# A cheaper elu on ScalarE, the transposes' copies moved ahead, a third tile for v and earlier weight loads in a two-layer kernel

## The chip, the cores and the metric

The kernel runs on one core of a Trainium2 chip. A core has five engines with a queue of instructions each: TensorE (PE; its weight loads are shown apart as PEld), VectorE (DVE), ScalarE (ACT), GpSimd (POOL) and SyncE (SP), which here only issues transfers. DMA engines move the data between HBM and the core's memory SBUF; TensorE writes to a second memory, PSUM. The metric is the time of one execution in microseconds (us), as the median of several runs.

## The reference

The input x has 4 batches of 512 tokens with 128 numbers each. Two layers follow, each of the form `x = x + attention(norm(x)) * silu(experts(norm(x)))`. The change lies in the first layer. Its attention has 16 heads and goes over each batch in 8 segments of 64 tokens with a memory M and a normalizer Z carried from segment to segment:

```
scores = where(mask, -inf, q @ k.T * scale)
att_dot = softmax(scores) @ v
sq = elu(q) + 1;  sk = elu(k) + 1
att_mem = (sq @ M) / (sq @ Z.T)
M, Z = M + sk.T @ v, Z + sk.sum(rows)
out = (gate * att_mem + (1 - gate) * att_dot) @ Wo
```

`elu(x) + 1` is `exp(x)` for x below zero and `x + 1` above. The first layer's second half is a mixture of 8 experts, two of which each token uses, beside a shared one. The second layer has an attention over 16 phases and another mixture of 8 experts.

## The kernel before

All work is written out in Python for one core, and every engine carries it out in the written order: the helpers `act1`, `vec1`, `mm1` and `pool1` put an instruction at the place in its engine's queue where the program calls them. So an instruction that waits holds up everything behind it on its engine.

`load_first` (L119 to L166) issues the first loads. The 16 tiles of x go out first, four on ScalarE's queue and twelve on SP's; the experts' weights wg, wu and wd and then the attention's weights follow on SP's. `norm_ffn0` (from L386) makes the norms and runs the first layer's experts; it lasts until about 78 us.

`attn0` (from L579) is the first attention. It runs over 32 segments, 8 for each of the 4 batches. q and k are produced by `project` for four segments at a time, in chunks: a chunk is 16 matmuls into one PSUM bank (`pp`), copied out by ScalarE (`pj`); v takes four chunks (`pv`), copied to a tile `vt` (by VectorE for the first two groups, by ScalarE later), sent to DRAM as `vd` and read back in another layout as `vone`. The tiles `vt` come from a pool with two buffers, so the third copy waits until the first transfer has landed.

In iteration n of the main loop (the two lists below are the order on the engines):

- TensorE: `sc` (scores of segment n+1), `mm` (memory of n), `tn` (transposes: the attention of n-2 and elu(k) of n+1), `mu` (memory's update of n), `dot` (weights of n times v), then up to four chunks of `pp` or `pv`, or, in each fourth segment, the output projection `po`.
- DVE: `E` (scores capped, L666), `rm` and `t` (memory divided, L723 and L724), `elu` of q(n+1) (L689), `mz` (memory's update, L758), `rd` twice, `t` (attention divided) and `sums` (L777, L723, L724, L780), `elu` of k(n+2) (L689).
- ScalarE: exp and Relu of q(n+1) (`elu_exp`), four copies `attT` and one `sk` out of `tn`, exp and Relu of k(n+2), the copy of the first chunk, the exponential of `E`, the copies of the other chunks.
- POOL: `t` times the gate (L743), `t` times the other gate (L781), the sum of both (L782); after each output projection, the addition to x (L809).

PSUM holds four double banks that `sc`, `mm`, `tn`, `mu`, `dot` and the chunks take in turn. So each of them waits until what stood in its bank four places earlier has been copied out.

elu is made of three instructions: ScalarE makes exp(x) and max(x, 0), and DVE adds min(exp(x), 1) and max(x, 0) in one. In the last segment of a batch (n = 7, 15, 23, 31) the memory isn't updated, so that k has no elu there and there is no `mu` and no `mz`.

From segment 18 on, the loop also carries steps of the second layer's experts for the first two batches (`between`): norm sums in 18 and 19, a square root on ScalarE in 20 with a table load on either side of it, the scaled tiles `xn` in 20 and 21, routing in 23 to 25. Chunks end with segment 25; segments 26 to 31 have none.

Of the kernel before, what the change touches and what calls it, by code (L numbers as in the profile page):

```python
# [12 lines left out]
F32 = mybir.dt.float32  # L13
# [3 lines left out]
AF = mybir.ActivationFunctionType  # L17
ALU = mybir.AluOpType
# [3 lines left out]
P = 128  # L22
B, S, D = 4, 512, 128
# [3 lines left out]
NT = 16  # L27
# [81 lines left out]
class Kernel:  # L109
# [8 lines left out]

    def load_first(self, pool, pool_attn, crossed=False):  # L119
        nc, i = self.nc, self.i  # L120
        for n in range(NT):
            eng = nc.scalar if n in (1, 3, 5, 7) else nc.sync
            eng.dma_start(out=self.x[:, n, :], in_=self.tiles_of(i["L0_attn_x"], n))

        self.wr = pool.tile([P, NE], F32, name="wr")
        nc.gpsimd.dma_start(out=self.wr, in_=i["L0_ffn_Wr"])
        self.ebias = pool.tile([P, NE], F32, name="ebias")
        nc.gpsimd.dma_start(out=self.ebias, in_=i["L0_ffn_expert_bias"].partition_broadcast(P))
        self.sg = pool.tile([P, 128], F32, name="sg")
        nc.gpsimd.dma_start(out=self.sg, in_=i["L0_ffn_Sg"])  # L130
        self.su = pool.tile([P, 128], F32, name="su")
        nc.gpsimd.dma_start(out=self.su, in_=i["L0_ffn_Su"])
        self.sd = pool.tile([P, D], F32, name="sd")
        nc.gpsimd.dma_start(out=self.sd, in_=i["L0_ffn_Sd"])
        self.wg = pool.tile([P, NE, F0], F32, name="wg")
        nc.sync.dma_start(out=self.wg, in_=i["L0_ffn_Wg"].rearrange("e d f -> d e f"))
        self.wu = pool.tile([P, NE, F0], F32, name="wu")
        nc.sync.dma_start(out=self.wu, in_=i["L0_ffn_Wu"].rearrange("e d f -> d e f"))
        self.wd = pool.tile([P, NE // 2, D], F32, name="wd")
        nc.sync.dma_start(  # L140
            out=self.wd, in_=i["L0_ffn_Wd"].rearrange("(j e) f d -> (e f) j d", e=2)
        )

        self.wqkv = []
        for w in ("Wq", "Wk", "Wv"):
            t = pool_attn.tile([P, H0 * DK], F32, name=f"l0{w}")
            nc.sync.dma_start(out=t, in_=i[f"L0_attn_{w}"])
            self.wqkv.append(t)
        self.wo = pool_attn.tile([P, H0, D], F32, name="l0wo")
        for p in range(2):  # L150
            nc.sync.dma_start(
                out=self.wo[p * 64 : p * 64 + 64],
                in_=i["L0_attn_Wo"].rearrange("(c v) d -> v c d", v=DK),
            )
        be = i["L0_attn_betas"][0, :, 0].rearrange("(hp a p) v -> a p hp v", a=2, p=2)
        self.gate = pool_attn.tile([P, 4, 2, DK], F32, name="gate")
        for p in range(2):
            for a in range(2):


                for x in range(2):
                    rows, cols = (a, slice(x, 4, 2))
                    if crossed:
                        rows, cols = (a + x) % 2, slice(2 * a, 2 * a + 2)
                    nc.sync.dma_start(
                        out=self.gate[rows * 64 : rows * 64 + 64, cols, p, :],  # L166
                        in_=be[a, p, x:4:2].partition_broadcast(64),
                    )
# [410 lines left out]
    def attn0(self, xnT, g0, stack, between):  # L579
# [4 lines left out]
        nc, tc = self.nc, self.tc  # L584
# [4 lines left out]
        pool = stack.enter_context(tc.tile_pool(name="a0", bufs=2))  # L589
# [9 lines left out]
        for k in range(4):  # L599
            t = pool.tile([P, 4, 2, DK + 1], F32, name=f"vone{k}", bufs=1)  # L600
            nc.gpsimd.memset(t[:, :, :, DK : DK + 1], 1.0)
            vone.append(t)
        qkv, vd, attT, seg = {}, {}, {}, {}
        wide = self.wide

        def project(h):


            if h >= 2 * B:
                return []  # L610
            qkv[h] = dst = [
                pool.tile([P, 32, 64], F32, name=f"pj{h}_{wi}", tag=f"pj{wi}")
                for wi in range(2)
            ]
            vd[h] = drams.tile([2, P * 16, DK], F32, name=f"vd{h}", tag="vd")
            def chunk_v(p, k):
                ps = self.narrow(f"pv{h}_{p}_{k}")
                self.mm1(
                    ps, lhsT=xnT[h // 2][:, h % 2 * 2 + p, :],
                    rhs=self.wqkv[2][:, k * S : (k + 1) * S], start=True, stop=True,  # L620
                )
                t = pool.tile([P, S], F32, name=f"vt{h}_{p}_{k}", tag="vt")
                if h > 1:
                    self.act1(t, ps, AF.Copy)
                else:
                    self.vec1(nc.vector.tensor_copy(t, ps))
                nc.sync.dma_start(
                    out=vd[h][p].rearrange("(q k c) d -> k q (c d)", k=2, c=8)[k], in_=t
                )

            def chunk(wi, cq):
                ps = self.narrow(f"pp{h}_{wi}_{cq}").rearrange("p (c k) -> p c k", c=4)
                for c4 in range(4):
                    c = cq * 4 + c4
                    for p in range(2):
                        self.mm1(
                            ps[halves[p], c4, :],
                            lhsT=self.wqkv[wi][:, c * 64 : c * 64 + 64],
                            rhs=xnT[h // 2][:, h % 2 * 2 + p, :], start=True, stop=True,
                        )  # L640
                view = dst[wi].rearrange("d k (t c) -> d (k t) c", c=16)
                self.act1(
                    view[:, :, cq * 4 : cq * 4 + 4], ps.rearrange("d c k -> d k c"), AF.Copy
                )
            qk = [(lambda wi=wi, cq=cq: chunk(wi, cq)) for wi in (1, 0) for cq in range(4)]
            v = [(lambda p=p, k=k: chunk_v(p, k)) for p in range(2) for k in range(2)]
            return v + qk if h else qk[:4] + v + qk[4:]

        def blocks(n, w):
            s = n % 4  # L650
            return qkv[n // 4][w][:, s * 8 : s * 8 + 8, :]
# [24 lines left out]
        def last(n):  # L676
            return n % 8 == 7

        def elu_exp(n, w):
            t = pool.tile([P, 8, 64], F32, name=f"elu{w}{n}", tag=f"elu{w}")  # L680
            up = pool.tile([P, 8, 64], F32, name=f"up{w}{n}", tag="up")
            self.act1(t, blocks(n, w), AF.Exp)
            self.act1(up, blocks(n, w), AF.Relu)
            seg[n][w] = t, up

        def elu(n, w):

            t, up = seg[n][w]
            self.vec1(nc.vector.scalar_tensor_tensor(t, t, 1.0, up, ALU.min, ALU.add))  # L689
            seg[n][w] = t  # L690
# [18 lines left out]
        def values(n):  # L709

            for p in range(2):
                src = vd[n // 4][p].rearrange("(s hp r) d -> s r hp d", s=4, hp=4)
                nc.sync.dma_start(out=vone[n % 4][:, :, p, 0:DK], in_=src[n % 4])
# [120 lines left out]
        for n in range(nseg):  # L834
            if n % 4 == 3:
                todo = project((n + 1) // 4 + 1)
            elif n == 0:
                todo = ahead
            each = 2 if n == 0 else 4 if n < 3 or n % 4 != 2 else 0
            nxt = n + 1 < nseg  # L840
            more = nxt and not last(n + 1)
            if n + 2 < nseg:
                values(n + 2)
            if nxt:
                elu_exp(n + 1, 0)
                scores(n + 1)
            memory(n)
            if nxt:
                elu(n + 1, 0)
            if n > 1 or more:  # L850
                turned(n - 2 if n > 1 else None, n + 1 if more else None)
            if not last(n):
                update(n)
            for f, *args in between.get(n - 0.5, []):
                f(*args)
            attend(n)
            ahead = n + 2 < nseg and not last(n + 2)
            if ahead:
                elu_exp(n + 2, 1)
            chunks, todo = todo[:each], todo[each:]  # L860
            for chunk in chunks[:1]:
                chunk()
            if nxt:
                scores_exp(n + 1)
            if ahead:
                elu(n + 2, 1)
            for chunk in chunks[1:]:
                chunk()
            for f, *args in between.get(n - 0.25, []):
                f(*args)  # L870
            if n % 4 == 2 and n > 4:
                output(n // 4 - 1)
            if not nxt:
                turned(n - 1)
            for f, *args in between.get(n, []):
                f(*args)
# [1611 lines left out]
```

## Time and profile before

| | us |
|---|---|
| median of 3 runs | 711.25 (709.93 to 712.07) |
| profiled execution | 715.14 |
| its span in the profile | 713.4 |
| TensorE busy | 667.3 |
| VectorE busy | 498.2 |
| ScalarE busy | 488.8 |
| GpSimd busy | 342.5 |

The span is divided, roughly, into the first layer's experts (to 78 us), the first attention (78 to 318), the second layer's experts (318 to 425) and its attention (425 to 713). A line of the profile names the engine, the line of the kernel and the tiles (`out<-in`), with busy time and mean duration in ns. Where the helpers record an operation, the line is that of the helper (L336 for all matmuls, L339 for all of ScalarE's activations), so these are told apart by their tiles. A releaser (`<-`) is what ended an idle time. Instructions of one engine overlap a little: a VectorE instruction shown with 0.69 us lets the next begin after about 0.61.

### The profile page before, as it was taken

What the parts mean: (1) busy time and instruction counts of PE and PEld (TensorE: products, weight loads), DVE (VectorE), ACT (ScalarE), POOL (GpSimd) and SP (SyncE); (2) the same over time, 40 slices, a digit from 0 to 9 for tenths busy, and PEclk for the clock granted to TensorE, in tenths of its full rate; (3) what the DMA queues carried; (4) which work ended last, traced back from release to release, by engine and by line L of the source; (5) the groups of instructions that cost most, each with busy time, mean ns of one, the idle gap of its engine ahead of it and who ended that gap; (6) DMA issues with size and microseconds to landing.
All of it is one profiled execution on the core that took longest, in us unless ns stands there. A gap on an engine that the chain in (4) does not pass through costs nothing.

```text
span 713.4 us, 23787 instructions
## 1 busy us (share of the span) xinstructions
PE 667.3 (94%) x10128; PEld 414.4 (58%) x10131; DVE 498.2 (70%) x1078; ACT 488.8 (69%) x809; POOL 342.5 (48%) x381
## 2 busy tenths in 40 slices
PE   7999899999999799789999999999999999999994
PEld 3666667977977668667777774332335243422433
DVE  5876475675677658864379125889897999588854
ACT  3423477786886977643453369989977999899830
POOL 7670046667667475783653243312482753312240
PEclk9999999999999998999999999999999999999998
DMA  7740152232232121100034159877949484965200
GB/s 159 162 137 0 49 161 83 58 107 77 62 103 78 51 81 43 33 3 1 1 120 155 52 170 259 206 186 168 238 144 217 125 233 143 216 149 125 60 17 19
DMA packets 84849, 79.46 MB, mean 111 GB/s; under 512 B 42512, under 2 KB 73520, under 8 KB 81664
## 3 DMA queue, kind: packets, MB, share of 16 engines
q1 hardware_dynamic: 81904, 75.12, 40.1%
q0 software_dynamic: 2256, 2.47, 1.8%
q8 instruction: 82, 1.34, 0.8%
q10 hardware_dynamic: 576, 0.26, 0.2%
q14 instruction: 31, 0.25, 0.1%
HBM read 51.62 MB, written 26.21 MB: 109 GB/s over the span
## 4 chain that ended last, share of the span: by engine, by line
PE 67%; ACT 14%; DVE 12%; DMA 3%; issue 2%; SPq 1%; ACTq 0%; DVEq 0%
PE acc L336 10%; ACT e L339 8%; PE eo L336 7%; PE pp L336 6%; PE po L336 6%; PE ph L336 4%; PE b L336 4%; PE s L336 3%; PE pl L336 3%; PE pg L336 2%; PE pu L336 2%; PE den L336 2%; PE pv L336 2%; DMA vd<-vt 2%; PE sc L336 2%
## 5 line engine op out<-in xcount | busy, mean ns | idle before, releaser
L339 ACT ACTIVATE e<-s 128x1024 f32<-128x1024 f32 x124 | 121.9, 1055 | 13.6 <-PE s L336 12.4
L336 PE MATMUL acc<-e,strip 128*32 128x512 f32 x1000 | 124.0, 598 | 0.9 <-DVE e L1885 0.9
L339 ACT ACTIVATE e<-e 128x1024 f32<-128x1024 f32 x104 | 107.3, 1094 | 0.0
L743 POOL TENSOR_TENSOR t<-t,gate 128x512 f32<-128x512 f32 x32 | 50.2, 1568 | 54.7 <-DVE t L724 54.7
L336 PEld LDWEIGHTS acc<-e,strip 128*32 128x32 f32 x1000 | 28.5, 109 | 69.9 <-issue 58.7
L781 POOL TENSOR_TENSOR t<-t,gate 128x512 f32<-128x512 f32 x32 | 49.6, 1551 | 33.9 <-DVE sums L780 27.1
L689 DVE SCALAR_TENSOR_TENSOR elu<-elu,up 128x512 f32<-128x512 f32 x60 | 46.2, 770 | 11.0 <-ACT up L339 10.8
L339 ACT ACTIVATE pj<-pp 128x512 f32<-128x512 f32 x64 | 37.8, 610 | 14.6 <-PE pp L336 13.5
L339 ACT ACTIVATE h<-ph 128x1024 f32<-128x1024 f32 x20 | 20.5, 1024 | 39.7 <-PE ph L336 32.3
L336 PE MATMUL s<-q,k 64*128 64x512 bf16 x256 | 40.9, 382 | 3.5 <-ACT e L339 3.3
L782 POOL TENSOR_TENSOR t<-t,t 128x512 f32<-128x512 f32 x32 | 42.6, 1332 | 2.5
L336 PEld LDWEIGHTS <-k 64*128 64x128 bf16 x256 | 8.8, 94 | 59.6 <-issue 57.7
L666 DVE TENSOR_TENSOR E<-sc,cap 128x512 f32<-128x512 f32 x32 | 22.0, 688 | 28.7 <-PE sc L336 28.7
L336 PE MATMUL eo<-w_out,h 128*128 128x128 f32 x320 | 39.7, 278 | 0.0
L336 PEld LDWEIGHTS eo<-w_out,h 128*128 128x128 f32 x320 | 37.6, 192 | 3.4 <-issue 2.2
L339 ACT ACTIVATE elu<-pj 128x512 f32<-128x512 f32 x60 | 38.6, 643 | 0.1
L1725 POOL TENSOR_TENSOR pr<-pr,pr 128x512 f32<-128x512 f32 x14 | 22.6, 1631 | 33.0 <-DVE pr L1720 32.9
L339 ACT ACTIVATE up<-pj 128x512 f32<-128x512 f32 x60 | 38.4, 640 | 0.0
L336 PE MATMUL pp<-xnT,l0Wk 128*64 128x128 f32 x512 | 32.2, 282 | 2.8 <-ACT sk L339 2.0
L339 ACT ACTIVATE attT<-tn 128x128 f32<-128x128 f32 x100 | 19.5, 283 | 21.6 <-PE tn L702 20.8
L1168 POOL TENSOR_SCALAR th<-th 128x512 f32<-128x512 f32 x4 | 3.4, 840 | 63.9 <-ACT th L339 63.9
L1634 DVE TENSOR_TENSOR second<-second,first 128x1024 f32<-128x1024 f32 x16 | 27.0, 1694 | 9.3 <-DMA second<-qf 9.3
(337 smaller groups left out, 1625.8 us busy)
## 6 DMA issues: line engine op xcount, KB each, us to landing
vd<-vt SPq DMA_DIRECT2D x32, 256.0 KB
vone<-vd SPq DMA_DIRECT2D x64, 128.0 KB
first<-qe SPq DMA_DIRECT2D x8, 1024.0 KB
second<-qf SPq DMA_DIRECT2D x16, 512.0 KB
third<-qf SPq DMA_DIRECT2D x32, 256.0 KB
qf<-qT SPq DMA_DIRECT2D x64, 64.0 KB
k<-kd SPq DMA_DIRECT2D x16, 256.0 KB
q<-qd SPq DMA_DIRECT2D x16, 256.0 KB
```

What stands on the lines that cost most here:

```text
L336: return self.pin(self.nc.tensor.matmul(*args, **kw))
L339: return self.pin(self.nc.scalar.activation(*args, **kw))
L666: self.vec1(nc.vector.tensor_tensor(e, ps[:, :, 0:256].rearrange("p x (hp c) -> p x hp c", hp=4), bc(bc(self.cap, 1, 4), 1, 2), ALU.min,))
L689: self.vec1(nc.vector.scalar_tensor_tensor(t, t, 1.0, up, ALU.min, ALU.add))
L743: nc.gpsimd.tensor_mul(t, t, self.gate)
L781: nc.gpsimd.tensor_mul(t, t, gate2)
L782: nc.gpsimd.tensor_add(t, t, seg[n]["t1"])
L1168: self.pool1(self.nc.gpsimd.tensor_scalar(t, t, 0.5, 0.5, ALU.mult, ALU.add))
L1634: self.vec1(self.nc.vector.tensor_mul(t, t, self.first1[mm][:, two]))
L1725: self.nc.gpsimd.tensor_add(self.prod1[b, m], self.prod1[b, m], t)
```

## The change

Five things are changed:

- In `load_first`, the tiles 8 to 15 of x are issued behind wg and wu.
- `vt` has three buffers.
- For segments 2 to 26 (`short`), elu is made differently: DVE takes min(x, 0) into the tile (`elu_low`), ScalarE makes its exponential in place, and DVE adds max(x, 0) in one instruction. Relu on ScalarE falls away, and one instruction on DVE is added.
- The order changes. On DVE the minimum of q(n+1) stands ahead of `E`, that of k(n+2) behind the first `t`; the closing elu of q(n+1) moves from behind the first `t` to behind `sums`, right ahead of the elu of k(n+2). On ScalarE `attT` and `sk` come first, then the exponential of q(n+1); the exponential of k(n+2) comes behind that of `E`.
- For the other segments (0, 1 and 27 to 31) elu is made as before, but the exp and Relu of q(n+1) also come behind `attT` and `sk`, and those of k(n+2) behind the exponential of `E`.

TensorE's and POOL's instructions and their order stay as they are.

```diff
@@ load_first
-        for n in range(NT):
-            eng = nc.scalar if n in (1, 3, 5, 7) else nc.sync
-            eng.dma_start(out=self.x[:, n, :], in_=self.tiles_of(i["L0_attn_x"], n))
+        def tokens(first, end):
+            for n in range(first, end):
+                eng = nc.scalar if n in (1, 3, 5, 7) else nc.sync
+                eng.dma_start(out=self.x[:, n, :], in_=self.tiles_of(i["L0_attn_x"], n))
+        tokens(0, 8)
...
         self.wu = pool.tile([P, NE, F0], F32, name="wu")
         nc.sync.dma_start(out=self.wu, in_=i["L0_ffn_Wu"].rearrange("e d f -> d e f"))
+        tokens(8, NT)
         self.wd = pool.tile([P, NE // 2, D], F32, name="wd")
@@ chunk_v
-                t = pool.tile([P, S], F32, name=f"vt{h}_{p}_{k}", tag="vt")
+                t = pool.tile([P, S], F32, name=f"vt{h}_{p}_{k}", tag="vt", bufs=3)
@@ attn0
+        def short(n):
+            return 1 < n < 27
+
+        def elu_low(n, w):
+            if short(n):
+                seg[n][w] = pool.tile([P, 8, 64], F32, name=f"elu{w}{n}", tag=f"elu{w}")
+                self.vec1(nc.vector.tensor_scalar_min(seg[n][w], blocks(n, w), 0.0))
+
         def elu_exp(n, w):
+            if short(n):
+                self.act1(seg[n][w], seg[n][w], AF.Exp)
+                return
             t = pool.tile([P, 8, 64], F32, name=f"elu{w}{n}", tag=f"elu{w}")
...
         def elu(n, w):
 
+            if short(n):
+                t = seg[n][w]
+                self.vec1(nc.vector.scalar_tensor_tensor(t, blocks(n, w), 0.0, t, ALU.max, ALU.add))
+                return
             t, up = seg[n][w]
             self.vec1(nc.vector.scalar_tensor_tensor(t, t, 1.0, up, ALU.min, ALU.add))
...
@@ the loop
+            ahead = n + 2 < nseg and not last(n + 2)
+            if nxt:
+                elu_low(n + 1, 0)
+                scores(n + 1)
+            memory(n)
+            if ahead:
+                elu_low(n + 2, 1)
+            if n > 1 or more:
+                turned(n - 2 if n > 1 else None, n + 1 if more else None)
             if nxt:
                 elu_exp(n + 1, 0)
-                scores(n + 1)
-            memory(n)
-            if nxt:
-                elu(n + 1, 0)
-            if n > 1 or more:
-                turned(n - 2 if n > 1 else None, n + 1 if more else None)
+                if not short(n + 1):
+                    elu(n + 1, 0)
             if not last(n):
                 update(n)
...
             attend(n)
-            ahead = n + 2 < nseg and not last(n + 2)
-            if ahead:
-                elu_exp(n + 2, 1)
+            if nxt and short(n + 1):
+                elu(n + 1, 0)
...
             if nxt:
                 scores_exp(n + 1)
             if ahead:
+                elu_exp(n + 2, 1)
                 elu(n + 2, 1)
```

## The prediction

> **What bounds the kernel now.** I read the page's busy shares first, then the stages, then the chain that ended last, and then the instructions in order of time in the stages that the change touches.
>
> The page's first part: TensorE is busy 94% of the span, so work taken from ScalarE pays only where TensorE waits for it.
>
> ```profile
> PE 667.3 (94%) x10128; PEld 414.4 (58%) x10131; DVE 498.2 (70%) x1078; ACT 488.8 (69%) x809; POOL 342.5 (48%) x381
> ```
>
> The busy time by stage (columns: length, then PE, PEld, DVE, ACT, POOL). The first row is four segments of the first attention: TensorE idles 0.6 us, DVE has 7.6 us free, POOL 7.5. In the second, where the next layer's norms join in, TensorE idles 5.7; in the third, the last segments, 4.9.
>
> ```profile
> 138.00:165.00 27.00, 26.42 (x754) 22.66 (x756) 19.36 (x42) 21.67 (x53) 19.46 (x14) 1.00 0.30 82
> ...
> 219.00:254.00 35.00, 29.32 (x776) 23.17 (x772) 25.86 (x71) 26.01 (x58) 19.37 (x16) 1.00 0.25 66
> ...
> 288.00:318.00 30.00, 25.11 (x777) 21.66 (x774) 23.25 (x51) 16.03 (x44) 24.49 (x18) 0.94 0.09 21
> ```
>
> Waits from 103 to 291 us (total, times, longest): TensorE waits for ScalarE 8.2 us in all, half of it for the copy of sk. That is what the relief of ScalarE can bring at most.
>
> ```profile
> PE pp L336 <- ACT sk L339: 4.1, 6, 2.1
> PE dot L336 <- ACT vt L339: 2.7, 3, 1.4
> ```
>
> One plain segment on DVE and on POOL. Start to start gives what each costs in a row: E 0.61, rm 0.30, t 0.61, elu 0.60, mz 0.60, rd 0.19 and 0.24, t 0.61, sums 0.08, elu 0.60. POOL's products show 1.66 us where they begin under an elu, against 1.29 elsewhere: after the elu has ended they need 1.13.
>
> ```profile
> 155.82 0.69 DVE L666 TENSOR_TENSOR E<-sc,cap 128x512 f32<-128x512 f32 x1 [1.61 <-PE sc L336]
> ...
> 158.97 0.69 DVE L724 TENSOR_TENSOR t<-dot,rd 128x512 f32<-128x512 f32 x1
> 159.58 0.17 DVE L780 TENSOR_TENSOR sums<-rd,sums 128x16 f32<-128x16 f32 x1
> 159.66 0.68 DVE L689 SCALAR_TENSOR_TENSOR elu<-elu,up 128x512 f32<-128x512 f32 x1
> 162.29 0.69 DVE L666 TENSOR_TENSOR E<-sc,cap 128x512 f32<-128x512 f32 x1 [1.95 <-PE sc L336]
> ```
>
> ```profile
> 157.50 1.66 POOL L743 TENSOR_TENSOR t<-t,gate 128x512 f32<-128x512 f32 x1 [0.76 <-DVE t L724]
> 159.81 1.67 POOL L781 TENSOR_TENSOR t<-t,gate 128x512 f32<-128x512 f32 x1 [0.65 <-DVE sums L780]
> 161.55 1.29 POOL L782 TENSOR_TENSOR t<-t,t 128x512 f32<-128x512 f32 x1
> ```
>
> What decides this forecast: DVE instructions with tensors in SBUF alone, back to back, while POOL has products to do. A tensor_scalar of 0.34 us takes 1.46 behind the product at 248.34, and the elu at 298.03 takes 1.61 behind that at 297.82. POOL gets in between two such DVE instructions.
>
> ```profile
> 246.79 0.34 DVE L945 TENSOR_SCALAR xn<-x,mv,rstd 128x128 f32<-128x128 f32 x1
> 246.93 1.33 POOL L781 TENSOR_TENSOR t<-t,gate 128x512 f32<-128x512 f32 x1 [4.84 <-DVE t L724]
> 248.26 1.46 DVE L945 TENSOR_SCALAR xn<-x,mv,rstd 128x128 f32<-128x128 f32 x1
> 248.34 1.29 POOL L782 TENSOR_TENSOR t<-t,t 128x512 f32<-128x512 f32 x1
> ...
> 297.82 1.27 POOL L782 TENSOR_TENSOR t<-t,t 128x512 f32<-128x512 f32 x1
> 298.03 1.61 DVE L689 SCALAR_TENSOR_TENSOR elu<-elu,up 128x512 f32<-128x512 f32 x1
> ```
>
> At the start, TensorE waits 2.12 us for wg, which is issued at 8.94 behind twelve tiles of x; the chain holds this transfer for 4.98 us.
>
> ```profile
> 13.96 2.03 PE L336 MATMUL pg<-xnT,wg 128*128 128x512 f32 x2 [2.12 <-DMA wg<-in_L_ffn_Wg_dram]
> ...
> 14.00:17.50 3.50, 3.50 (x5) 1.27 (x6) 1.79 (x6) 0.64 (x2) 1.46 (x3) 0.51 1.11 243
> ```
>
> **The change, part by part.** The profiled execution took 715.14 us (span 713.4), 3.9 above the median of 711.25; the sum is made on the profile and carried over as a difference.
>
> *Weights sooner: -2.8.* Eight issues of 0.65 us leave SP's queue ahead of wg, which is then issued at 3.75 instead of 8.94 and, at the 4.98 us it took, lands at about 8.7; wu 0.6 later. TensorE needs wg at 11.83, so its wait goes. Late next is DVE: parts until 14.17, hs until 14.77, the four xn until 15.79. Then the transposes (0.6) and pg for the second pair begin near 16.5 instead of 19.30. The eight tiles of x moved behind wg and wu go out from 5.0 to 10.2, and their first reader, at 19.67, comes to 17: covered by some 4 us. wd keeps its place as the fifteenth issue, at 10.2; its reader at 20.6 comes to 18. POOL's and ScalarE's queues keep their order. From 19 to 78 us the chain is TensorE without a gap, so the gain stays. Bounds: 2.1 (the wait alone) and 3.7 (all up to 17.64 but 1.9 of work); I take what DVE leaves. The granted clock of 0.51 from 14.0 to 17.5 follows a gap of only 2.12 us, so the half-rate stretch should go as well. The Trainium skill (TensorE: Matmul & The Clock Gate, What's actually happening) has the clock halve after an idle window of about 3.4 us; by that this gap would not have halved it, and the gain would be the wait alone, 2.1.
>
> *Elu by a minimum, in a plain segment.* For 25 q and 22 k (segments 2 to 26, k not in the last of a sequence) a Relu leaves ScalarE: 47 x 0.64 us, off the path except in the waits above. DVE gets 47 minima. The nearest row is the tensor_scalar at L595, 128x512 in SBUF: 0.43 us alone, some 0.35 in a row; behind a POOL product it waits up to 1.13 more. The elu of q now stands behind t, next to the elu of k and the next segment's minimum: three instructions in SBUF in a row, while POOL has its product and sum of the same segment waiting. As at 246.79, POOL gets in after the first and after the second: elu q 0.60, product 1.13, elu k 0.60, sum 1.13, minimum 0.35, and only then E. The minimum of k, right behind t, goes ahead of POOL at 0.35. Per segment: 0.61+0.30+0.61+0.35+0.60+0.19+0.24+0.61+0.08+0.60+1.13+0.60+1.13+0.35 = 7.40 us. TensorE needs about 6.5 (four groups of pp 3.64, sc 0.62, mm 0.47, tn 0.64, mu 0.63, dot 0.47). So DVE becomes the bound. Without k (segments 5, 13) it is 5.3 and I take 5.5; without mz (7, 15) 6.8. The ends for the two waits are 0 and 2.26; I take the upper one, since the xn row has the same pattern.
>
> The Trainium skill (SBUF — State Buffer, Who interferes with whom) says that whoever issues first holds the port pair for the whole instruction. Read as DVE's queue going first, a segment would cost 5.14 and TensorE stay the bound; the xn row shows POOL taking its turn.
>
> *Sum by segments.* Segment 0: q of segment 1 keeps exp and Relu but now behind the copy of sk, +0.35; the first minima and a sum ahead of E(2) bring it to +1.25. Segment 1: 7.4 against 6.06, +1.3. Segments 2 to 17, from E at 107.41 to 216.34: 12x7.40 + 2x6.80 + 2x5.5 = 113.4 against 108.9, +4.5; the third tile of v and the copies first are in this, their waits being covered now by DVE. Segment 18 (norm sums, in POOL's shadow): +0.4. Segments 19 to 26 (to 292.07) had ScalarE and DVE in turn on the chain: +1.7 in 19 and +1.1 in 25, where two or three minima and a wait of 1.13 come on top of a full DVE; -1.4, -1.7 and -0.5 in 20, 21 and 22 to 24, where the wait for v (1.4 at TensorE) and the copy of sk behind the table loads (2.06) go: -0.8.
>
> *Segments 27 to 31: +3.7.* Here q keeps exp and Relu, but they now stand behind attT (0.65 in a row) and sk (0.49): ready 2.35 us after tn, at 295.47 instead of the elu at 293.59. Behind that elu queue mz, rd, t, the elu of k, and tn of the next segment. E(29) comes 1.9 later, E(30) 2.9 (the late elu now meets POOL's product), E(31) 4.0; the last po 3.7.
>
> Sum: -2.8 +1.25 +1.3 +4.5 +0.4 -0.8 +3.7 = +7.55 on the profile, 722.7; carried to the median 711.25 + 7.55 = 718.8.
>
> **The rivals.** *POOL's turns cost nothing (faster).* Were the two waits 0, TensorE would stay the bound: -2.8 weights, -8.2 waits for ScalarE, +0.6 at the start, +2.0 minima on the full DVE in 19 to 26, +2.5 tail: -5.9, 705.4. For it: POOL is busy 72% in a plain segment and could have finished. Against: xn. It decides if the two waits together stay under 1.3 us per segment (6.5 less 5.14).
> *Gains and costs meet (same).* Were the two waits 0.83 us each, the products being under way already, a plain segment would take 6.8; twelve of them at 0.6 less give 711.6. For it: ScalarE may have exp of k late, so that the elu of k meets POOL's product halfway. Against: the sum then waits behind that elu in full, ahead of the minimum.
> *The clock (slower still).* DVE-bound, TensorE idles near 0.9 us per segment. If that lets the clock drop as at 14.0, each 3.4 us at half costs up to 1.7; four of them make 725.5. Against: gaps of 0.7 at 114 and 178 did not; from 266 to 273 it stood at 0.54.
> *The weights do nothing.* Were wg late for other reasons, 2.8 more on any case.
>
> **How the numbers follow.** Forecast 0.52 (714 to 723 by itself), faster rival 0.27, same 0.07, clock 0.14. Slower by over 0.3% (2.1 us, about what a measurement of this kernel tells from none) is 0.52 + 0.14. The range reaches from 705, the faster rival, to 726.
>
> **What would show it.** Right: E to E near 7.4 us in plain segments, elu of k and the minimum of q with means far above 0.68 and 0.43, DVE on the chain from 100 to 290; E(29) to E(31) 5.5 to 6.5 apart; pg at 11.9 without a wait. Wrong: po still every 26.5 us with minima at 0.43 on the mean.

## The result and the profile after

The changed kernel takes 721.53 us (718.53 to 721.84, 4 runs) against 710.59 (709.89 to 712.07, 4 runs) for the kernel before: a ratio of 1.0133, 95% interval 1.0109 to 1.0157. It is slower by some 10.9 us in the median (9.5 by the ratio); the forecast was 718.8 with a range from 705 to 726. The profiled execution took 721.83 us, with a span of 720.1.

Busy time in the same four plain segments' stage as before, then in the last segments (columns: length, PE, PEld, DVE, ACT, POOL, granted clock, DMA share, GB/s):

```profile
138.00:165.00 27.00, 25.45 (x714) 21.28 (x714) 25.79 (x46) 16.62 (x43) 18.88 (x13) 1.00 0.30 81
...
300.00:330.00 30.00, 23.08 (x652) 20.06 (x650) 19.84 (x43) 15.68 (x41) 17.99 (x15) 0.77 0.05 12
```

The window is the same, but the changed kernel gets less done in it (714 matmuls for 754). ScalarE has 5 us less to do there, DVE went from 19.4 of 27 us to 25.8, and TensorE lost a microsecond. The page's chain, by engine, says the same of the whole span: DVE held 12% of it before.

```profile
PE 58%; DVE 25%; ACT 14%; issue 2%; DMA 1%; DVEq 0%; SPq 0%; ACTq 0%
```

The page's groups of the closing elu and of the minimum (busy us, mean ns of one) show that the DVE time is mostly not work. Alone they take 0.68 and 0.42 us.

```profile
L704 DVE SCALAR_TENSOR_TENSOR elu<-pj,elu 128x512 f32<-128x512 f32 x47 | 48.9, 1054 | 7.2 <-ACT elu L342 7.2
L688 DVE TENSOR_SCALAR elu<-pj 128x512 f32<-128x512 f32 x47 | 36.9, 784 | 0.5 <-ACT pj L342 0.5
```

One plain segment on DVE in order of time (start, duration), and then on POOL:

```profile
156.86 0.68 DVE L669 TENSOR_TENSOR E<-sc,cap 128x512 f32<-128x512 f32 x1
...
158.36 0.42 DVE L688 TENSOR_SCALAR elu<-pj 128x512 f32<-128x512 f32 x1
...
160.34 0.17 DVE L798 TENSOR_TENSOR sums<-rd,sums 128x16 f32<-128x16 f32 x1
160.43 0.68 DVE L704 SCALAR_TENSOR_TENSOR elu<-pj,elu 128x512 f32<-128x512 f32 x1
161.39 1.40 DVE L704 SCALAR_TENSOR_TENSOR elu<-pj,elu 128x512 f32<-128x512 f32 x1 [0.28 <-ACT elu L342]
162.71 1.51 DVE L688 TENSOR_SCALAR elu<-pj 128x512 f32<-128x512 f32 x1
164.15 0.68 DVE L669 TENSOR_TENSOR E<-sc,cap 128x512 f32<-128x512 f32 x1
```

```profile
160.57 1.67 POOL L799 TENSOR_TENSOR t<-t,gate 128x512 f32<-128x512 f32 x1 [0.65 <-PE pp L339]
162.32 1.62 POOL L800 TENSOR_TENSOR t<-t,t 128x512 f32<-128x512 f32 x1
```

DVE and POOL take turns: elu of q, POOL's product, elu of k, POOL's sum, the minimum, and only then E. The product ends at 162.24 and elu of k at 162.79; the sum ends at 163.94 and the minimum at 164.22. E to E is 7.29 us here. The step at the start came too; pg begins without a wait, and the second pair 3.2 us earlier than before:

```profile
11.28 1.02 PE L339 MATMUL pg<-xnT,wg 128*128 128x512 f32 x2
...
16.09 1.02 PE L339 MATMUL pg<-xnT,wg 128*128 128x512 f32 x2
```

### The profile page after: what moved, and what is told of

The parts are those of the page before. It is cut to its first block, busy times and chain, and to the rows that moved or that the text cites. A ratio compares the mean times of both kernels' runs of the same rounds, so it can differ in the third digit from the quotient of the medians.

```text
span 720.1 us, 23825 instructions
## 1 busy us (share of the span) xinstructions
PE 669.9 (93%) x10128; PEld 418.6 (58%) x10131; DVE 546.7 (76%) x1125; ACT 466.1 (65%) x762; POOL 345.8 (48%) x381
## 4 chain that ended last, share of the span: by engine, by line
PE 58%; DVE 25%; ACT 14%; issue 2%; DMA 1%; DVEq 0%; SPq 0%; ACTq 0%
PE acc L339 10%; ACT e L342 8%; PE eo L339 7%; DVE elu L704 4%; PE po L339 4%; PE pp L339 4%; PE ph L339 4%; DVE elu L688 4%; DVE t L742 3%; PE s L339 3%; PE b L339 3%; PE pl L339 3%; DVE E L669 2%; PE pg L339 2%; PE den L339 2%
## 5 line engine op out<-in xcount | busy, mean ns | idle before, releaser
L761 POOL TENSOR_TENSOR t<-t,gate 128x512 f32<-128x512 f32 x32 | 43.7, 1367 | 73.4 <-DVE t L742 73.4
L799 POOL TENSOR_TENSOR t<-t,gate 128x512 f32<-128x512 f32 x32 | 51.2, 1601 | 29.0 <-DVE sums L798 20.7
L704 DVE SCALAR_TENSOR_TENSOR elu<-pj,elu 128x512 f32<-128x512 f32 x47 | 48.9, 1054 | 7.2 <-ACT elu L342 7.2
L800 POOL TENSOR_TENSOR t<-t,t 128x512 f32<-128x512 f32 x32 | 48.1, 1505 | 2.5
L1748 POOL TENSOR_TENSOR pr<-pr,pr 128x512 f32<-128x512 f32 x14 | 22.6, 1635 | 32.0 <-DVE pr L1743 32.0
L688 DVE TENSOR_SCALAR elu<-pj 128x512 f32<-128x512 f32 x47 | 36.9, 784 | 0.5 <-ACT pj L342 0.5
L339 PEld LDWEIGHTS po<-l0wo,attT 64*128 64x128 f32 x512 | 31.6, 200 | 3.6 <-issue 2.4
L339 PE MATMUL po<-l0wo,attT 64*128 64x128 f32 x512 | 33.0, 287 | 0.6 <-DVE t L742 0.6
L339 PE MATMUL dot<-vone,E 64*64 64x65 f32 x1024 | 24.1, 237 | 9.9 <-DVE E L669 7.4
```

The costliest lines, as they stand in the source:

```text
L339: return self.pin(self.nc.tensor.matmul(*args, **kw))
L688: self.vec1(nc.vector.tensor_scalar_min(seg[n][w], blocks(n, w), 0.0))
L704: self.vec1(nc.vector.scalar_tensor_tensor(t, blocks(n, w), 0.0, t, ALU.max, ALU.add))
L761: nc.gpsimd.tensor_mul(t, t, self.gate)
L799: nc.gpsimd.tensor_mul(t, t, gate2)
L800: nc.gpsimd.tensor_add(t, t, seg[n]["t1"])
```

## The experiments

The theory of the prediction: in a plain segment DVE is the bound, because POOL's product and its sum get in between DVE instructions that stand in a row and have their tensors in SBUF. The rivals: the minima cost by their work alone; ScalarE's new order makes the exponentials late. Beside these stands the question what each of the other parts is worth. All ratios are to the kernel before on the same chip; the kernel before took 708.4 to 712.8 us on the chips used, so times of different runs are best compared by their ratios. "A plain segment" is the usual distance from one E to the next where k has an elu, and E(2) to E(18) are sixteen segments: 108.5 us in the profile before, 113.8 in the changed kernel.

**POOL's product and sum left out of the changed kernel.** The gate on the second part and the memory part are then missing.

```
-            nc.gpsimd.tensor_mul(t, t, gate2)
-            nc.gpsimd.tensor_add(t, t, seg[n]["t1"])
```

> The changed kernel with POOL's second product and its sum left out of every segment of the first attention, so that the attended values lack the gate on the second part and the whole memory part. DVE and ScalarE keep all their work and their order. Theory (DVE is held by POOL's turns between elu of q, elu of k and the minimum): elu of k and the minimum go back to 0.6 to 0.7 and 0.35 to 0.45 us, plain segments to TensorE's 6.5 us instead of 7.28, and the total falls by 12 x 0.78 in segments 2 to 17 and 2 to 4 in 19 to 31, some 11 to 13 us: 709. Rival (the 47 minima as work, or the later exponential, hold the segment): plain segments stay at 7.0 or above and the total above 717.

Measured: 703.90 us (699.37 to 708.24, 8 runs), ratio 0.9904 (0.9873 to 0.9934). DVE has all its 47 minima and ScalarE its new order. The groups of DVE from 80 to 340 us:

```profile
L704 DVE SCALAR_TENSOR_TENSOR elu<-pj,elu 128x512 f32<-128x512 f32 x47 | 32.2, 695 | 11.5 <-ACT elu L342 11.4
L688 DVE TENSOR_SCALAR elu<-pj 128x512 f32<-128x512 f32 x47 | 19.6, 418 | 0.9 <-ACT pj L342 0.9
```

The means fell from 1054 and 784 to 695 and 418 ns. Most plain segments take 6.4 to 6.5 us, E(2) to E(18) 106.6. So POOL's two instructions are what DVE was held by. Against the changed kernel's ratio of 1.0133 this is 2.3%, some 16 us, more than the 11 to 13 expected: E(18) to E(27), where 2 to 4 had been allowed for all that follows, fell by 7.4 us.

**The exponential of k back in its place.**

```
+            if ahead:
+                elu_exp(n + 2, 1)
             if nxt and short(n + 1):
                 elu(n + 1, 0)
...
             if ahead:
-                elu_exp(n + 2, 1)
                 elu(n + 2, 1)
```

> The changed kernel with the exponential of k put back to its place of before, ahead of the chunk of the projection and of the scores' exponential on ScalarE. Rival (the elu of k is late because its exponential is late: 0.28 us of its 1.40 show that wait): plain segments fall from 7.28 by 0.3 to 0.6, the total by 5 to 9 us. Theory (POOL's turn behind elu of q ends after the exponential anyhow): plain segments 7.2 to 7.35, total within 2 us of 721.5.

Measured: 721.87 us (717.20 to 724.94, 4 runs), ratio 1.0131 (1.0086 to 1.0175), plain segments 7.27 to 7.29, but for one of 8.08. The wait of 0.28 us that the trace puts down to the exponential lies inside POOL's turn and is worth nothing. For the exponential of k this rival is out; the rest of ScalarE's order is tried by itself further down.

**The minimum of q behind E.**

```
             if nxt:
-                elu_low(n + 1, 0)
                 scores(n + 1)
+                elu_low(n + 1, 0)
```

> The changed kernel with one edit: the minimum of q goes from ahead of E to just behind E, both neighbours then reading PSUM; elu of q and elu of k stay next to each other. Theory: of the two turns of 1.13 us the second is no longer in a chain of SBUF-only instructions, E begins behind elu of k: 5.14 + 1.13 = 6.27, again TensorE's 6.47; E(2) to E(18) 104 to 107, total 711 to 714. If POOL's sum still comes ahead of E or slows the minimum behind it, 6.6 to 7.0 and 715 to 718. Rival (work of DVE or the order on ScalarE): 7.2, 721.

Measured: 711.98 us (710.10 to 718.22, 10 runs), ratio 1.0002 (0.9977 to 1.0027). One line moved gives back the whole loss against the kernel before: the same instructions, one turn of POOL less. Nine of the twelve plain segments take 6.5 to 6.8 us, the other three 7.9 to 8.2 (7.5 to 7.8 in the kernel before); E(2) to E(18) is 108.4, a little over what was expected. In its timeline the closing elu of k, which has waited for POOL's product, is followed by E, which reads PSUM and isn't held by the sum:

```profile
157.91 1.40 DVE L704 SCALAR_TENSOR_TENSOR elu<-pj,elu 128x512 f32<-128x512 f32 x1 [0.29 <-ACT elu L342]
158.84 1.62 POOL L800 TENSOR_TENSOR t<-t,t 128x512 f32<-128x512 f32 x1
159.52 0.69 DVE L669 TENSOR_TENSOR E<-sc,cap 128x512 f32<-128x512 f32 x1 [0.21 <-PE sc L339]
160.13 0.61 DVE L688 TENSOR_SCALAR elu<-pj 128x512 f32<-128x512 f32 x1
```

E runs from 159.52 to 160.21 while the sum runs until 160.46.

**The elu of q behind mz.**

```
             if not last(n):
                 update(n)
+            if nxt and short(n + 1):
+                elu(n + 1, 0)
...
             attend(n)
-            if nxt and short(n + 1):
-                elu(n + 1, 0)
```

> The changed kernel with one edit: the closing elu of q goes from behind the scaled values to just behind the memory update mz, between two DVE instructions that read PSUM. The same instructions, the same exponential, one SBUF-only neighbour less for elu of k. Theory: in a plain segment elu of k begins right behind sums, POOL's product then takes its turn, the minimum of q is the last to wait: 5.14 + 1.13 = 6.27 us, TensorE's 6.47 becomes the bound. E(2) to E(18) falls from 113.8 to 104 to 106, the total by 8 to 10 us: 712. Rival (it is the sum of DVE's work, or the exponential of q behind the copies, which now holds mz too): 7.2 or more a segment, total 720 or above.

Measured: 730.29 us (726.40 to 731.35, 4 runs), ratio 1.0228 (1.0182 to 1.0274): by the ratios some 7 us slower than the changed kernel where 8 to 10 faster was expected. Segments alternate between some 6.66 and 7.95 us. In the short ones elu of q takes 1.16 us behind POOL's first product, which that place had not been reckoned to meet, and the minimum 1.49: 5.14 + 0.48 + 1.06. In the long ones elu of k comes 0.3 us too late, so that the product has already begun; it and the minimum behind it then both wait:

```profile
156.20 1.27 POOL L799 TENSOR_TENSOR t<-t,gate 128x512 f32<-128x512 f32 x1 [1.73 <-DVE sums L798]
156.42 1.59 DVE L704 SCALAR_TENSOR_TENSOR elu<-pj,elu 128x512 f32<-128x512 f32 x1 [0.28 <-ACT elu L342]
...
157.55 1.60 POOL L800 TENSOR_TENSOR t<-t,t 128x512 f32<-128x512 f32 x1
157.94 1.49 DVE L688 TENSOR_SCALAR elu<-pj 128x512 f32<-128x512 f32 x1
```

The theory's rule "neighbours in a row" was too narrow. What counts in these rows is whether POOL has an instruction under way or waiting when an SBUF-only DVE instruction comes up, whatever stands before it.

**The tail in the old order.** The exponential, Relu and elu of q stand ahead of the transposes again where the old form is kept (n + 1 = 1 and 27 to 31).

```
             if nxt:
+                if not short(n + 1): elu_exp(n + 1, 0)
                 elu_low(n + 1, 0)
                 scores(n + 1)
             memory(n)
+            if nxt and not short(n + 1): elu(n + 1, 0)
...
-            if nxt:
+            if nxt and short(n + 1):
                 elu_exp(n + 1, 0)
-                if not short(n + 1):
-                    elu(n + 1, 0)
```

> The changed kernel with the exponential, Relu and elu of q put back ahead of the transposes for the segments that keep the old form (n = 1 and 27 to 31). Theory: E(27) to E(31) goes from 26.4 back to 20.9 plus 0.5 (E(29) 1.9, E(31) 4 us sooner), E(2) 0.3 to 1 us sooner: total 716 to 717. Rival (the tail is long because POOL is behind from the segments before): E(27) to E(31) 25 or more, total 721.

Measured: 716.01 us (714.55 to 719.37, 10 runs), ratio 1.0055 (1.0035 to 1.0075). E(27) to E(31) takes 22.6 us for 26.4; the last three steps are 4.56, 5.37 and 4.77 as before. The first, E(27) to E(28), takes 7.90 us against 6.28 in the kernel before, so that 22.6 stands where 21.4 was expected. In the main this term was what it was said to be; what holds that first step is not shown.

**Both repairs together** (the two edits above in one kernel).

> The changed kernel with the minimum of q behind E and the old order for q in the segments that keep the old elu: the two repairs measured alone gave 9.5 us (721.5 to 712.0) and 5.5 (to 716.0). They are in different segments, so they add: 706 to 707. What is then left over the 701.9 of weights and three tiles alone (about 5 us) is elu of q and elu of k next to each other and the minima where DVE is full (segments 19 to 26). If the repairs overlap: 709 to 711.

Measured: 704.69 us (703.16 to 707.82, 4 runs), ratio 0.9937 (0.9911 to 0.9962). They add within the interval: the two ratios, 1.0002 and 1.0055 against 1.0133, would give 0.9924. (The expected 706 to 707 us were for a chip on which the kernel before takes 712; here it takes 708.4.)

**The weights' loads alone, on the kernel before.**

```
-        for n in range(NT):
+        tokens(0, 8)
...
         nc.sync.dma_start(out=self.wu, ...)
+        tokens(8, NT)
```

> The kernel before with the weights' loads sooner and nothing else. Theory (the weights' term stands by itself): pg begins at 11.3 to 11.9 us without a wait for wg, the second pair's pg near 16.1 instead of 19.3, and everything behind is 3.0 us earlier: 707.5 us, ratio 0.996. Rival (the gain is lost again before the end, because later stages wait for something that does not move): 710 to 711.

Measured: 709.88 us (707.32 to 711.74, 10 runs), ratio 0.9966 (0.9942 to 0.9990). The trace has pg at 11.44 and 16.24 instead of 13.96 and 19.30, what follows until 110 us is some 3.0 us earlier, and the stretch at half rate is gone:

```profile
14.00:17.50 3.50, 3.29 (x20) 2.37 (x21) 3.35 (x10) 1.69 (x4) 1.17 (x2) 1.00 1.07 286
```

How much of this is the load's is less sure than it looks. The next run leaves the loads as they were and waits for wg as long, but its trace has no half-rate stretch behind that wait:

```profile
13.58 1.13 PE L336 MATMUL pg<-xnT,wg 128*128 128x512 f32 x2 [2.09 <-DMA wg<-in_L_ffn_Wg_dram]
...
14.00:17.50 3.50, 3.41 (x21) 2.07 (x20) 2.35 (x7) 1.19 (x2) 1.18 (x3) 1.00 1.04 252
```

The first chunk of the attention begins there at 76.94 us, 1.7 earlier than in the profile of the kernel before (78.63), and at 75.57 in the run with the weights alone. So up to half of the 3.0 us goes with a stretch that one execution with this wait had and another had not.

**Three tiles for v alone, on the kernel before.**

```
-   name=f"vt{h}_{p}_{k}", tag="vt")
+   name=f"vt{h}_{p}_{k}", tag="vt", bufs=3)
```

> The kernel before with three tiles for v and nothing else. Theory: TensorE's six waits for vt and dot in the first attention (2.7 us) shrink, some of it is taken up by the copy of sk, which is next in line: 1 to 2 us faster, 709 us. Rival (v hidden anyway, the wait is for the transfer and not for the tile): 710.6, no change.

Measured: 703.54 us (702.48 to 704.32, 4 runs), ratio 0.9899 (0.9871 to 0.9927), some 7 us by the ratio where 1 to 2 were expected (of TensorE's waits for the copies of v, of which the row in the prediction has three, not six). The row that would have told it stands in the trace before, with ScalarE and not with TensorE. Copies of v in the kernel before, and the total of such waits from 103 to 291 us:

```profile
118.42 0.63 ACT L339 ACTIVATE vt<-pv 128x512 f32<-128x512 f32 x1
119.42 0.64 ACT L339 ACTIVATE vt<-pv 128x512 f32<-128x512 f32 x1
121.18 0.60 ACT L339 ACTIVATE vt<-pv 128x512 f32<-128x512 f32 x1 [1.13 <-DMA vd<-vt]
123.17 0.60 ACT L339 ACTIVATE vt<-pv 128x512 f32<-128x512 f32 x1 [1.40 <-DMA vd<-vt]
```

```profile
ACT vt L339 <- DMA vd<-vt: 9.5, 8, 2.3
```

With three tiles:

```profile
ACT vt L339 <- DMA vd<-vt: 2.1, 4, 0.6
PE pp L336 <- ACT sk L339: 2.1, 1, 2.1
```

ScalarE stood still for 9.5 us, now for 2.1; TensorE's waits for the copy of sk, which stands behind the copies of v in ScalarE's queue, fell from 4.1 us to 2.1 with it. Segments that had 7.9, 8.2 and 8.8 us now have 6.5, 6.5 and 6.9.

**Weights and three tiles, on the kernel before** (both diffs above).

> The kernel before with the weights' loads sooner and three tiles for v, elu and the order of the copies untouched. The two gains are in different stages, so they add: 711.8 - 2.4 - 8.3 = 701. If instead part of the gain of three tiles was luck of one run or one chip: 704 to 706.

Measured: 701.94 us (701.58 to 704.63, 4 runs), ratio 0.9855 (0.9816 to 0.9894). The two add. This is the fastest kernel of the study, and it leaves elu and the order of the copies alone.

**The order alone: the changed kernel with the old elu everywhere.**

```
         def short(n):
-            return 1 < n < 27
+            return False
```

> The changed kernel with the old elu (exponential and Relu on ScalarE, no minima) in every segment; what is left of the change is the order (copies of the transposes first, elu of q behind them, exponential of k behind the scores'), three tiles for v and the weights. Theory: elu of q stands 2.35 us behind tn and mz, rd, t, elu of k and E behind it: 6.5 us a segment without a turn of POOL, 7.6 with one, as in segments 27 to 31 of the changed kernel; I expect 6.9 to 7.6 and a total of 712 to 720. Rival (the order is harmless as long as DVE has no minima): 6.5 a segment, only the tail's 4 to 5 on 702: 707.

Measured: 724.43 us (723.09 to 726.21, 4 runs), ratio 1.0226 (1.0198 to 1.0254), beyond the upper end expected. Between 80 and 330 us DVE waits for the Relu of the elus:

```profile
DVE elu L707 <- ACT up L342: 49.9, 35, 4.0
```

Over the ratio of weights and three tiles this is 3.8%, the largest cost of a part put in alone. The minima, put on top of it, win 0.9% back (1.0133 against 1.0226): without the Relu, elu of q is ready sooner, and DVE's waits for ScalarE ahead of the elus fall from 49.9 us to 14.1.

**The minima alone: weights, three tiles, ScalarE's old order, elu by a minimum.** The minimum of k stands behind E, that of q behind mz.

```
             scores(n + 1)
+            elu_low(n + 2, 1)
...
             update(n)
+            elu_low(n + 2, 0)
```

(The minimum of q(4) comes one iteration later than this, ahead of its exponential.)

> The kernel before with the weights sooner, three tiles for v and elu by a minimum, but ScalarE in its order of before (exponential of q ahead of the transposes, elu of q behind t), and each minimum put between DVE instructions that read PSUM: the one of k behind E, the one of q behind mz. Theory (the minima cost nothing as work; it was the order on DVE and ScalarE that cost): plain segments 6.47 us, E(2) to E(18) 104 to 105, total 701.9 less up to 2 for ScalarE's relief in segments 19 to 26, plus up to 2 for DVE being full there: 700 to 704. Rival (DVE's 33 us more of work are what cost): plain segments above 6.8, total 708 or more.

Measured: 716.38 us (714.55 to 717.34, 5 runs), ratio 1.0098 (1.0076 to 1.0120). The expectation of 700 to 704 failed; the minima cost 2.5% here. So the order alone costs 3.8%, the minima alone, in these places, 2.5%, and both together, as in the changed kernel, 2.8%: the two don't add. A segment on DVE, and the start of what TensorE waits for:

```profile
149.49 0.93 DVE L688 TENSOR_SCALAR elu<-pj 128x512 f32<-128x512 f32 x1
...
150.63 0.69 DVE L742 TENSOR_TENSOR t<-mm,rm 128x512 f32<-128x512 f32 x1
...
151.47 2.84 PE L339 MATMUL pp<-xnT,l0Wk 128*64 128x128 f32 x48 [0.45 <-DVE t L742]
...
152.44 0.90 DVE L688 TENSOR_SCALAR elu<-pj 128x512 f32<-128x512 f32 x1
...
154.52 1.09 PE L339 MATMUL pp<-xnT,l0Wk 128*64 128x128 f32 x16 [0.21 <-DVE sums L798]
155.54 0.70 PE L339 MATMUL sc<-pj,pj 64*64 64x64 f32 x32
156.31 0.69 DVE L669 TENSOR_TENSOR E<-sc,cap 128x512 f32<-128x512 f32 x1 [1.25 <-PE sc L339]
```

DVE is idle 1.25 us ahead of E, so it isn't full. But four PSUM banks go round: the first chunk of pp takes the bank of mm, which t empties, and the fourth takes that of dot, which the scaled values empty. A minimum that waits for POOL ahead of t delays TensorE's next matmul, and so the next E. From 104 to 222 us TensorE waits 7.3 us for t and sums, against 0.2 in the kernel with weights and three tiles alone; E(2) to E(18) is longer by 11.6 (116.1 for 104.5), so a part of the loss is not accounted for by these waits.

**Both minima behind elu of k, in the time in which DVE waits for the scores.**

```
             if ahead:
                 elu(n + 2, 1)
+            elu_low(n + 2, 0)
+            elu_low(n + 3, 1)
```

(The minima of k(2), k(4) and q(4) stand elsewhere.)

> The same as the run with the old order and the minima between PSUM readers, but with both minima (of q of the segment after next, of k of the one behind it) moved behind elu of k, into the 1.2 us in which DVE waits for the scores ahead of E (27.2 us in 17 times from 100 to 220 us in the kernel with the weights and three tiles alone). Theory (a minimum costs only where it delays t or the scaled values, which free the banks that the projection's matmuls take next): TensorE's waits for t and sums go, plain segments 6.5 to 6.8 us, E(2) to E(18) 104 to 109, total 701 to 707. Rival (two more SBUF-only instructions a segment cost their 0.9 us wherever they stand, because POOL is in the way): 7.2 or more, total 713 to 718.

Measured: 717.24 us (716.07 to 718.16, 5 runs), ratio 1.0059 (1.0045 to 1.0073); the theory's 701 to 707 failed and its rival came true. The DVE and POOL rows:

```profile
153.63 0.69 DVE L704 SCALAR_TENSOR_TENSOR elu<-pj,elu 128x512 f32<-128x512 f32 x1
154.23 2.92 DVE L688 TENSOR_SCALAR elu<-pj 128x512 f32<-128x512 f32 x2
157.08 0.68 DVE L669 TENSOR_TENSOR E<-sc,cap 128x512 f32<-128x512 f32 x1
```

```profile
153.78 1.67 POOL L799 TENSOR_TENSOR t<-t,gate 128x512 f32<-128x512 f32 x1 [0.65 <-DVE sums L798]
155.52 1.35 POOL L800 TENSOR_TENSOR t<-t,t 128x512 f32<-128x512 f32 x1
```

Two minima of 0.35 us take 2.92: each waits for one of POOL's instructions. The usual segment is 7.28 us again, to the hundredth what the changed kernel has, with other instructions in the same pattern. The idle time that DVE has ahead of E is the time in which POOL does its two. TensorE's waits for t and sums did fall, from 7.3 us to 2.0, as the theory said; but now DVE makes E late instead.

## Why the prediction was right, and where its sizes were off

The step that decided it held: POOL gets a turn behind elu of q and one behind elu of k, at 1.13 us as the row at 246.79 had it. Two of the prediction's readings are slightly off, and the forecast's sum uses neither: TensorE's waits for ScalarE add up to 8.5 us in that view, not 8.2, and the upper bound for the weights is 3.9 by its own figures, not 3.7. Forecast 7.40 us for a plain segment, measured 7.28; 6.8 without mz, measured 6.70; 5.5 without k, measured 6.14, where the same turns were only guessed at. The run without POOL's pair shows the cause by itself, and the run with the minimum behind E shows it with all work in place. The rule that the Trainium skill gives (SBUF — State Buffer, Who interferes with whom), read as DVE's queue going first, would have left these segments at 6.5; the measured 7.28 speaks against that reading, not against the rule that an instruction holds the ports whole.

The terms of the sum, from the two profiles, as what the changed kernel lost against the one before:

| Step | forecast | measured |
|---|---|---|
| Weights sooner | -2.8 | -3.2 |
| Third tile of v, before E(1) | not in the sum | -0.7 |
| Segment 0 | +1.25 | +2.2 |
| Segment 1 | +1.3 | +1.9 |
| Segments 2 to 17 | +4.5 | +4.1 |
| Segment 18 | +0.4 | +0.2 |
| Segments 19 to 26 | -0.8 | +2.9 |
| Segments 27 to 31, to the last po | +3.7 | +5.2 |
| Sum to the last po | +7.55 | +12.6 |

*Weights sooner.* The time fits: 2.4 us by the ratio of the run alone, 3.0 in its trace. But one premise is not borne out. The prediction took the half-rate stretch from 14.0 to 17.5 us as what a gap of 2.12 us brings; the run with three tiles alone has a gap of 2.09 and no such stretch. Set against that run, the first chunk comes 1.4 us sooner in the run with the weights alone and 2.0 sooner with weights and three tiles, which is nearer to the wait alone, 2.1, the estimate that the prediction made from the Trainium skill (TensorE: Matmul & The Clock Gate, What's actually happening). The rest of the 3.2 goes, in the main, with the half rate that the profile of the kernel before happened to have.

*Segments 19 to 26* is the term that failed. 19, 20, 21 and 25 came as told (+1.7, -1.6, -1.9, +1.2). "-0.5 in 22 to 24" came as +2.4, and 26, which had no price, as +1.1. Of the 2.4, 1.7 lie in segment 22 alone: 10.40 us for 8.73, with the clock at half from 255.2 to 258.6. In the run with the old tail the same instructions took 9.02 there, without such a stretch, so 1.4 of it goes with the clock. What made segment 26 longer is not shown; without POOL's pair it took 6.28 us, as in the kernel before, for 7.40.

*Segments 0 and 1* hold a stretch at half rate too, from 98.2 to 105.0 us; four chunks of pp take 5.41 us in it for 3.71.

```profile
98.20:105.00 6.80, 6.33 (x104) 5.94 (x106) 5.51 (x13) 2.67 (x5) 4.35 (x3) 0.50 0.25 80
```

*The tail.* E(29), E(30) and E(31) came 1.9, 3.1 and 4.4 us later against E(28), as told (1.9, 2.9, 4.0); the last po added 0.8 at half rate (313.2 to 323.5).

*The clock*, a rival at 0.14, came true in part beside the forecast: up to the last po 27.3 us at half rate against 13.7 before. The 1.4 us in segment 22, the 1.7 in the four chunks and the 0.8 in the last po come to 3.9 us, most of the 5 by which the sum to the last po was too low. What sets it off wasn't tried.

*From the profile to the median.* The lag of 12.6 us behind the last po is 6.7 at the end of the two profiled executions: some 3 us go in the second attention, and the end of the execution before held 7.2 us from DVE's last instruction on, that of the changed kernel 4.5. Nothing of the change is there, and the sum had nothing for it. From the last po to the end the profile of the kernel before takes 399.9 us, those with weights, three tiles or both 397.5 to 398.5, the changed kernel's 394.0, and the others lie from 392.4 to 398.8. So the profile of the kernel before is the longest of all there, but by only 1.4 to 2.4 us against its nearest relatives; what else moves these stages is not known. So that the total came within 2.7 us of the forecast is in part luck: the sum was 5 us too low up to the last po, and 6 us that it hadn't counted were given back behind it.

*What the sum didn't see.* "The third tile of v and the copies first are in this, their waits being covered now by DVE": in the changed kernel it can't be told apart, but the third tile alone was worth some 7 us. By ratios to the kernel before, weights and tile give -1.5%, the order then +3.8%, and the minima -0.9% on top of it. On the old order the minima cost +2.5%. The sum put the tile at nothing by itself, and so didn't see that the loss of the new elu and the new order is twice what the total shows: 2.8% against the kernel with weights and three tiles. The faster rival's 705.4, with POOL's turns at nothing, stands beside 703.9 measured with POOL's pair left out.

## What to carry to other kernels

Before work is moved to DVE, look at what POOL does at that moment: an instruction of DVE on SBUF alone costs its own time plus what is left of POOL's, however idle DVE looks on the mean. Read waits also on the engine that is not the bound: ScalarE's 9.5 us for a buffer stood behind some 7 us of the total, where TensorE's own row for v showed 2.7, and one more buffer took most of them. And price the parts of a change apart: here two of four were worth 10 us and the other two cost 20.

## What the runs showed of the hardware

In these traces POOL and DVE exclude each other by whole instructions where DVE has its tensors in SBUF (128x512, f32): a minimum of 0.42 us took up to 1.5 behind elu with one of POOL's instructions waiting, in the changed kernel and wherever it was moved to such a place; two took 2.92. Instructions that read PSUM keep their time under POOL (E 0.69 us, mz 0.69). A minimum between PSUM readers still took 0.90 to 0.93 while POOL's sum or product ran, and 0.42 where no POOL instruction was under way as it began, as at 158.36 in the changed kernel; so the place that costs it nothing isn't "between PSUM readers" but "when POOL is done". This exclusion has no entry in the list of waits: it shows as longer durations on both engines, 1.67 for 1.29 on POOL.

Up to the last po the granted clock went to half in stretches of 3.4 us or multiples of it. A gap of 2.12 us in TensorE had such a stretch behind it in the kernel before, a gap of 2.09 in the run with three tiles had none.
